# Ten of fourteen float32 LayerNorm tiles transposed by DMA, as two planes of 16 bits

## The chip, the cores and the metric

The kernel runs on one core of one Trainium2 chip. The metric is the time of one execution on the device, in microseconds (us), as a median over runs. A profiled execution gives the trace that the views below are read from: which instruction ran on which engine, and when. The engines are PE (the matrix engine, TensorE, with PEld for its weight loads), DVE (VectorE), ACT (ScalarE), POOL (GpSimd) and SP (SyncE, which here only issues DMAs). Each engine takes its instructions strictly in its own program order, so an instruction that waits holds back everything behind it on that engine.

## The reference: one decoder layer

The input `x` is 8 sequences of 112 tokens with 512 features in float32, 896 tokens together. Three blocks follow one another, each with a LayerNorm before it and a residual sum after it:

```
x = x + attn(layernorm(x))          # 16 heads of 32, causal, rotary q and k, float32
x = x + xattn(layernorm(x), ctx)    # 16 heads, keys and values from ctx (128 features)
x = x + ffn(layernorm(x))           # 512 -> 2 x 2048 -> 512, gelu gate, products in fp8 e4m3
```

with `layernorm(x) = (x - mean) / sqrt(var + 1e-5)` over the 512 features. Of the 375 context rows only the first 112 pass the causal mask, so only these are read.

## The kernel before: seven tiles of tokens, and an order written out

The 896 tokens are seven tiles of 128 rows. A product on PE contracts over the partitions, so the normalized tokens must be turned: a tile of 128 tokens x 512 features becomes four blocks of 128 features x 128 tokens. The result lies in two arrays, `fmh` and `fml`: the value rounded to the format fp32r, and the rest that the rounding left. Each product of the two attention blocks is then three products, high by high, high by low and low by high (`mm3`, line 363).

**LayerNorm.** `ln_stats` (lines 304 to 313) computes mean and variance on DVE, a power of -1/2 on POOL (line 307), and the normalized tile `xn` on ACT (kind "a", before self-attention, line 311) or on DVE (kinds "x", before cross-attention, and "f", before the feed-forward part, line 313). There are seven tiles of each kind, so "a" and "x" make the fourteen float32 tiles of the title.

**Turning a float32 tile.** For "a" and "x", PE multiplies the tile with an identity, four transposes of 128x128 into one bank of PSUM (line 349, tiles `xna` and `xnx`). `split_evac` then takes the bank out: ACT copies and rounds into `fmh` (line 324), and DVE subtracts to give `fml` (line 325).

**Turning an "f" tile.** Kind "f" is fp8 and is turned by a DMA already: `flip` widens to bfloat16 (line 332), SP issues a DMA transpose of 128x512 elements of 2 bytes (line 333, `xt<-xw`), and ACT or DVE narrows the result into `x8` (lines 334 and 335).

**The stages.** First the tiles are normalized and projected to values, queries and keys for tokens 0 to 447 and 448 to 895 (`values`, `proj_fm`, rotation in `rope_evac`). Self-attention runs sequence by sequence: scores on PE (line 420, `pss`), mask and maximum on DVE (429), exponentials with their sums on ACT (432), reciprocals on DVE (435), a scaling on POOL or DVE (436), a transpose of the probabilities on PE (443, `pspt`), a copy (320, `pts`), and the product with the values (453, `psav`). When all sequences of a token tile are through, `finish` does its output projection (`wo`), the residual sum on DVE (466) and the "x" LayerNorm. `cross_kv` makes keys and values of the context, `cross_q` the queries of cross-attention in three groups of tokens, 0 to 383, 384 to 639 and 640 to 895, with the weights `wxq`. Cross-attention has the same steps as self-attention, then `wxo`, the "f" LayerNorm, and the feed-forward part in four groups of tokens (`psfg` line 572, `psfo` line 597).

**The order.** All these steps are first collected in a list and then issued in the order that the string `ORDER` gives by their numbers; a letter behind a number chooses the engine (a ACT, d DVE, p POOL) where a step may run on more than one. So stages overlap as that order has it, and PE works on output projections and context keys between the small products of attention. `CAPS` gives the number of buffers of each kind; the SP queue holds all loads and, further on, the DMAs of the rotation and the transposes.

```
        def tr():
            for c in range(4):
                o, x = ps()[:, c * 128 : (c + 1) * 128], xn()[:, c * 128 : (c + 1) * 128]
                T.transpose(o, x, ident())
        op("pe", tr, r=[xn, ident], w=[ps])
        split_evac(lambda k: fm[k]()[:, :, t0:t1], lambda k: K(fm[k], t0, t1), [ps], psv, 512)
```

Of the kernel before, what the change touches and what calls it, by code (L numbers as in the profile page):

```python
# [8 lines left out]
F32 = mybir.dt.float32  # L9
FR = mybir.dt.float32r  # L10
BF = mybir.dt.bfloat16
F8 = mybir.dt.float8e4
# [19 lines left out]
PAIR = 4  # L32

# [17 lines left out]
class Plan:  # L51
# [47 lines left out]
    "p": 8, "s": 4, "t": 15, "w": 4, "w8": 1, "sm": 12, "m": 4, "pt": 1, "av": 1, "ws": 4, "pts": 7, "fg": 6, "fo":  # L99
    2, "rp": 5, "xn": 3, "f": 5, "cx": 3, "P": 4, "a8": 1, "nw": 20, "warm": 1, "vt": 2,  # L100
}
ORDER = """
1 23-24 37 40 25-26 43 46 85-87 94 22 88 0 89 95-98 2-20 90-91 21 38 103 112 39p 99 41 42p 92 100-101 44 113 104 102
114 105 45d 106 93 107 257-258 272-273 259 274 47 275-276 32 28 49 115 29 311 116 48p 277 260 278 108 50 261 279-282
262 109 263 283 320 51d 312 264-267 55 35 52 36 56 117 110 287 53 73 58 284 111 57d 64 118-119 288-290 268 120 59 54d
321 60d 74 75p 65 27 61 286 269 66d 302 322 62 63d 313 303-304 323 305 67 33 76 30 70-71 68 72p 155 291 156-157
121-122 158 123 159 292 124-129 160 130 161-163 131 189 132 190 164 191 165 293 192 294 193-194 324 134 133 1128 544
34 31 271 285 136 166-167 170 135 195 295 168 69d 196 296 197 297 138-139 198 140 199 141-142 298 200 143 172 202 299
201 144 173 145 174 146-147 175 148 545 77 169 1129 546p 314-315 306 223 176-177 149 178-180 224 240 225 547 82 325
137p 78d 151 150 153 83 316 307 171p 152 204 270 241 181-183 185 184 242 326 226-227 243 228 530 327-328 154d 528-529  # L110
203 187 186 244 229 206 230 245 231-232 246 548 233 207 247 234 248-249 236 235 250 308 208 309 209-210 317 211 318
212-215 310 188d 205p 329 216 251-253 330-333 217 334-335 219 319 218 237-238 254 79 255 220-221 336 465-469 337 470
346-347 338 348-349 339 350-352 340 353 471-472 354 473 355 474 356-357 256d 239d 341-342 222d 380 475 397 476 398 359
80 565 477 84d 358 360 592 361 343 549p 1130p 527 362p 81p 300 363-366 399 580 578 478-479 594 582 608 584 606 566 570
596 367-369 602 604 568 572 590 593 609 567 381 510 382 511 370-371 512 383 372 513-516 373-374 569 573 571 574
375-376 517-521 400 384 401 385 402 607 597 605 579 583 603 522 575d 585 581 591 595 617 576 414 386 586 587p 577a 523
377 301 344 524 378 415 387-388 588 416 403 389 610 618 598 620 622 599d 624 630 611d 634 623 589a 417 390-391 418 600
419 404 420 405-406 421 407 392 636 601d 621 635 619 625 612 422-423 408 424-425 631 626 642 632 393 646 654 637 633
643 613a 658 660 638 648 647 649 659 409-410 345p 627p 379p 639p 431 448 432 628 629a 655 614 394-395 644-645 427 426
650 656 412 428 411 429 640 449 433-434 450 435 615 531 651p 641d 657 661 690 616 721 662 693 663p 652 695 697 691 727  # L120
653a 698 480 436-438 481 439 664 482 451-454 483 455-457 440 458 441-442 484-485 459 731 729 719 709 715 733 707 703
692 665d 696 694 705 699 710 728 722 720 708 732 706 704 525 413p 700d 717-718 701 702a 716 666 763 430p 443-444 711
712p 460 667 723 462-463 550 446 445 668 724p 396p 713 730 734 714a 768 461 735 766 769 486 1139-1141 1142a 788 767
1135 725 726a 736p 1136-1137 1143 487-488 1144-1145 792 764 794 770-771 765 778 776 780 790 1138d 772 489 737 495 490
496 491 497 464p 773p 447p 779 777 738a 804 782 795 800 802 806 783 781 492 793 789 791 784 807 803 801 805 774 739
836 775d 1146d 796 853 855 851 785p 786 797p 841 787d 837 808 498 669 499-500 670 501 798 740 854 852 856 842 849
843-844 838 879 799d 877 875 839-840 880 850 526 809p 671 502 672 503-504 673-675 810 676 505 677 506 678-679 845 873
865 861 811a 846p 867 857 863 741 876 864 874 868 866 878 862 858p 847 909 812 507 848d 912 493-494 508-509 553 556
532 859 916 869 914 928 881 922 870p 917 913 860a 742-743 680 744 926 745 871 746-747 681 910 813 915 927 551 936-937
923 911 872d 934 940 814 924 682 882p 918 748-751 883 752 815 753 816-826 884a 935 925 929 533 754 946-947 941 950 930  # L130
# [49 lines left out]
2131 1971-1972 2125a 2139a 2140 2101 2145 2116 2144 2117-2118 2148d 2146d 2108 2119 1973d 1981p 2120a 2126 2127a 2128  # L180
2147 1974d 2149 2142 2150 2121d 2143 2129 2109 2130 2132d 2133 2134a 2135-2136 2046-2048 2110 2049 2050a 2051d
2111-2112 2113a 2151-2152 2158-2161 2153-2154 2114d 2162a 1982 1975 2115 2122 2045 2163p 2164 2052 2165-2168 2155d
2156d 2169a 2170d 2157 2171
"""
QG = ((0, 4), (4, 8))
XQ = ((0, 384), (384, 640), (640, 896))
# [474 lines left out]
```

## Time and profile before

| | us |
|---|---|
| median of 3 runs | 281.81 (281.14 to 282.51) |
| the profiled execution: its time | 281.24 |
| its span, first to last instruction | 279.3 |
| PE busy | 273.7 (98%) |
| DVE busy | 221.8 (79%) |
| ACT busy | 194.3 (70%) |
| POOL busy | 109.5 (39%) |
| transposes of the float32 tiles, line 349: 56 products | 8.4 busy |
| DMA transposes of the "f" tiles: 7 | 2.4 each from issue to landing |

A busy sum adds the durations of the records of one engine. Matmuls are pipelined, so records of PE overlap, and a PE that shows as busy throughout need not be at its peak: what a product costs is read from the chain of waits, where consecutive products follow each other at the pace at which PE really takes them. The granted clock of PE was 0.998 of full speed over the whole execution.

### The profile page before, as it was taken

What the parts mean: (1) busy time and instruction counts of PE and PEld (TensorE: products, weight loads), DVE (VectorE), ACT (ScalarE), POOL (GpSimd) and SP (SyncE); (2) the same over time, 40 slices, a digit from 0 to 9 for tenths busy, and PEclk for the clock granted to TensorE, in tenths of its full rate; (3) what the DMA queues carried; (4) which work ended last, traced back from release to release, by engine and by line L of the source; (5) the groups of instructions that cost most, each with busy time, mean ns of one, the idle gap of its engine ahead of it and who ended that gap; (6) DMA issues with size and microseconds to landing.
All of it is one profiled execution on the core that took longest, in us unless ns stands there. A gap on an engine that the chain in (4) does not pass through costs nothing.

```text
span 279.3 us, 7540 instructions
## 1 busy us (share of the span) xinstructions
PE 273.7 (98%) x2648; PEld 223.6 (80%) x2648; DVE 221.8 (79%) x909; ACT 194.3 (70%) x697; POOL 109.5 (39%) x123
## 2 busy tenths in 40 slices
PE   8999999999999999999999999999999999999994
PEld 3788988898888888878999887888888887776654
DVE  3896887889988889897897889998967858565372
ACT  3854410787999999970599999999886864633141
POOL 2727680347796398614035454732201200101000
PEclk9999999999999999999999999999999999999999
DMA  7994322332030413016909609410010100001005
GB/s 229 362 339 158 137 104 87 113 129 76 17 104 26 153 40 115 2 35 43 102 9 87 69 3 105 49 38 4 2 40 2 38 2 0 20 1 41 0 38 190
DMA packets 18742, 21.70 MB, mean 78 GB/s; under 512 B 7056, under 2 KB 11536, under 8 KB 18704
## 3 DMA queue, kind: packets, MB, share of 16 engines
q1 hardware_dynamic: 15584, 18.07, 20.1%
q0 software_dynamic: 3120, 3.15, 12.7%
q8 instruction: 21, 0.34, 0.5%
q14 instruction: 17, 0.14, 0.2%
HBM read 22.39 MB, written 1.84 MB: 87 GB/s over the span
## 4 chain that ended last, share of the span: by engine, by line
PE 92%; DVE 4%; ACT 1%; DMA 1%; issue 0%; POOL 0%; POOLq 0%
PE psm L363 44%; PE psfg L572 18%; PE pspt L443 10%; PE psfo L597 9%; PE pss L420 6%; PE psav L453 5%; PE psm L349 2%; DVE fml L325 1%; DMA x_sb<-in_x_dram 1%; DVE wxqwl L283 1%; DVE v_sb L320 0%; DVE lnx L304 0%; ACT xna L311 0%; ACT wvwh L281 0%; DVE xnx L313 0%
## 5 line engine op out<-in xcount | busy, mean ns | idle before, releaser
L432 ACT ACTIVATE P<-P,at 112x112 f32<-112x112 f32 x256 | 96.5, 381 | 8.3 <-DVE at L429 8.1
L436 POOL TENSOR_TENSOR P<-P,at 112x448 f32<-112x448 f32 x52 | 48.5, 938 | 52.6 <-DVE at L435 35.8
L429 DVE CUSTOM_DVE_ANT_0 P<-pss,mask 112x112 f32<-112x112 f32 x256 | 55.7, 265 | 3.5 <-PE pss L420 2.2
L432 ACT ACTIVATION_READ_ACCUMULATOR P<-P,at 112x1 f32 x256 | 48.7, 190 | 0.0
L443 PE MATMUL pspt<-ident,P 112*112 112x112 f32 x256 | 35.9, 262 | 0.0
L443 PEld LDWEIGHTS pspt<-ident,P 112*112 112x112 f32 x256 | 27.5, 133 | 7.6 <-issue 1.2
L572 PE MATMUL psfg<-x,wgwl 128*128 128x256 fp8e4 (+1 forms) x256 | 28.5, 259 | 0.0
L572 PE MATMUL psfg<-x,wgwh 128*128 128x256 fp8e4 (+1 forms) x256 | 28.0, 259 | 0.0
L572 PEld LDWEIGHTS <-wgwl 128*128 128x128 fp8e4 x256 | 21.9, 98 | 5.0 <-issue 1.4
L572 PEld LDWEIGHTS <-wgwh 128*128 128x128 fp8e4 x256 | 22.1, 98 | 4.5 <-issue 0.9
L320 ACT CAST gf<-psfg 128x512 bf16<-128x512 f32 x34 | 18.6, 585 | 9.0 <-PE psfg L572 9.0
L320 DVE CAST gf<-psfg 128x512 bf16<-128x512 f32 x22 | 15.0, 685 | 9.3 <-PE psfg L572 9.3
L582 DVE TENSOR_TENSOR gf<-gf 128x512 bf16<-128x512 bf16 x28 | 12.4, 453 | 12.2 <-ACT gf L580 8.3
L320 ACT COPY pts<-pspt 112x448 f32<-112x448 f32 x36 | 18.9, 526 | 4.2 <-PE pspt L443 2.2
L429 DVE DVE_READ_ACCUMULATOR2_ANT at<- 112x1 f32 x256 | 21.3, 83 | 0.0
L580 ACT ACTIVATE gf<-gf 128x512 bf16<-128x512 bf16 x28 | 16.6, 631 | 5.5 <-DVE gf L320 5.4
L320 DVE COPY pts<-pspt 112x448 f32<-112x448 f32 x28 | 17.3, 617 | 2.2 <-PE pspt L443 2.0
L307 POOL TENSOR_TENSOR lnf<-lnf,mhalf 128x1 f32<-128x1 f32 x7 | 4.1, 585 | 37.0 <-DVE lnf L306 37.0
L420 PE MATMUL pss<-k,q 32*112 32x112 f32 x512 | 16.9, 268 | 0.0
L420 PEld LDWEIGHTS pss<-k,q 32*112 32x112 f32 x512 | 14.0, 172 | 3.1 <-issue 2.0
L320 ACT CAST ob<-psfo 128x512 bf16<-128x512 f32 (+1 forms) x7 | 3.5, 494 | 18.3 <-PE psfo L597 18.3
L597 PE MATMUL psfo<-wlin,a 128*128 128x512 fp8e4 x64 | 15.6, 379 | 0.0
(140 smaller groups left out, 644.4 us busy)
## 6 DMA issues: line engine op xcount, KB each, us to landing
qt<-qs SPq DMA_DIRECT2D x32, 112.0 KB, 2.0
x_sb<-in_x_dram SPq DMA_DIRECT2D x7, 256.0 KB, 4.9
out_dram<-x_sb SPq DMA_DIRECT2D x6, 256.0 KB, 2.3
wst<-in_Wv_dram SPq DMA_DIRECT2D x4, 256.0 KB, 4.9
wst<-in_Wq_dram SPq DMA_DIRECT2D x4, 256.0 KB, 5.1
wst<-in_Wo_dram SPq DMA_DIRECT2D x4, 256.0 KB, 3.7
wst<-in_Wk_dram SPq DMA_DIRECT2D x4, 256.0 KB, 5.1
wst<-in_WoutT_dram SPq DMA_DIRECT2D x4, 256.0 KB, 3.3
```

Source lines behind the costliest of these rows:

```text
L320: lambda e: A.copy(dst(), src()) if e == "act" else V.tensor_copy(dst(), src()), r=r, w=w)
L363: T.matmul(out=out(), lhsT=l(a), rhs=r(b), start=q == 0, stop=q == 3 * tot - 1)
L420: T.matmul(out=banks[r]()[:S, j * S : (j + 1) * S], lhsT=qk[0]()[rs, c, t0 : t0 + S], rhs=qk[1]()[rs, c, t0 : t0 + S], start=True, stop=True)
L429: op("dve", lambda ps=ps, r=r, j=j, Pv=Pv, sm=sm: V.tensor_tensor_reduce(Pv()[:, r, :], ps()[:S, j * S : (j + 1) * S], mask(), -SCALE, BIG ...
L432: op("act", lambda r=r, Pv=Pv, sm=sm: A.activation(Pv()[:, r, :], Pv()[:, r, :], AF.Exp, bias=sm()[:S, r : r + 1], scale=-1.0, accum_out=s ...
L436: op(("pool", "dve"), lambda e, sm=sm, Pv=Pv: LO[e].tensor_tensor(Pv(), Pv(), sm()[:S, 8:12].unsqueeze(2).broadcast_to([S, 4, S]), ALU.mul ...
L443: T.transpose(pt()[:S, r * S : (r + 1) * S], Pv()[:, r, :], ident()[:S, :S])
L453: T.matmul(out=av()[r * 32 : (r + 1) * 32, c * S : (c + 1) * S], lhsT=v_sb()[:, b, h * 32 : (h + 1) * 32], rhs=pts()[:S, r * S : (r + 1) * ...
L572: T.matmul(out=ps()[:, j * n : (j + 1) * n], lhsT=wg()[i][:, c, (m + j) * 128 : (m + j + 1) * 128], rhs=x8()[:, c, t0:t1], start=(c == 0), ...
L580: op("act", lambda gb=gb: A.activation(gb()[:, :w], gb()[:, :w], AF.Gelu_apprx_tanh), w=[(gf, 0)])
L582: op("dve", lambda gb=gb, fb=fb: V.tensor_tensor(fb()[:, :w], gb()[:, :w], fb()[:, :w], ALU.mult), r=[(gf, 0)], w=[(gf, 1)])
L597: T.matmul(out=ps()[:, :wd], lhsT=a8()[:, m, s], rhs=wl()[0][:, m, hs], start=(m == 0), stop=(m == NH - 1))
```

## The change

A new function, `flip_x`, takes the place of the four products for the "a" tiles 4, 5 and 6 and for all seven "x" tiles. The "a" tiles 0 to 3 stay on PE. The DMA transpose is issued on elements of 2 bytes, as in `flip`, so the float32 tile is first split into its low and high halves:

- a copy on POOL or ACT sorts the 1024 halves of each row into two planes (`xl`),
- SP issues one DMA transpose of 128x1024 elements of 2 bytes (`xv`),
- a copy on ACT or DVE interleaves the two planes again to float32 (`xf`),
- a copy on ACT or POOL rounds into `fmh`,
- a subtraction on POOL or DVE gives `fml`.

The line numbers of the changed kernel for these steps are 352, 353, 354, 357 and 358; what was line 363 (`mm3`) is line 390 there.

`ORDER` is another string throughout: the steps that are in both kernels are issued in another sequence, and many that may run on two engines have another one. `FLIP = 0` leaves the second new function, `flip_p`, for the probabilities, without use, and `hl` and `xt` have no buffers.

```diff
+FLIPA = 4
+FLIP = 0
...
 CAPS = {
...
-1 23-24 37 40 25-26 43 46 85-87 94 22 88 0 89 95-98 2-20 90-91 21 38 103 112 39p 99 41 42p 92 100-101 44 113 104 102
...
+23 1 85-87 22 88 0 25 103 89 104-107 40 90 41 42p 2-18 91 19-21 108-109 24 43-44 94-97 45p 92 37 27 46 38 28 26 55 36
...
     def tmp(name, dt=F32, extra=()):
-        return Buf(("t", *extra), lambda k: sb.tile([128, 512], dt, tag=f"t{k['t']}", name=nm(name)))
+        return Buf(("t", *extra), lambda k: sb.tile([128, 1024 if dt == U16 else 512], dt, tag=f"t{k['t']}", name=nm(name)))
...
+    LO2 = {"act": A.copy, "dve": V.tensor_copy, "pool": G.tensor_copy}
...
+    def planes(t):
+
+        return t.bitcast(U16).rearrange("p (n two) -> p two n", two=2)
...
+    def flip_x(i, xn):
+
+        t0, t1 = i * 128, (i + 1) * 128
+        xl, xt, xf = tmp("xl", U16), tmp("xv", U16), tmp("xf")
+        two = lambda t: t().rearrange("p (two n) -> p two n", two=2)
+        op(("pool", "act"), lambda e: LO2[e](two(xl), planes(xn())), r=[xn], w=[xl])
+        op("sp", lambda: nc.sync.dma_start_transpose(xt().rearrange("p (g s) -> p g s", g=8), xl()), r=[xl], w=[xt])
+        op(("act", "dve"), lambda e: LO2[e](planes(xf()), two(xt)), r=[xt], w=[xf])
+        src = lambda: xf().rearrange("p (c s) -> p c s", c=4)
+        hi, lo = (lambda: fm[0]()[:, :, t0:t1]), (lambda: fm[1]()[:, :, t0:t1])
+        op(("act", "pool"), lambda e: LO2[e](hi(), src()), r=[xf], w=K(fm[0], t0, t1))
+        op(("pool", "dve"), lambda e: LO[e].tensor_tensor(lo(), src(), hi().bitcast(F32), ALU.subtract),
+           r=[xf, *K(fm[0], t0, t1)], w=K(fm[1], t0, t1))
+
     def layernorm(i, kind):
         xn = ln_stats(i, kind)
         if kind == "f":
             flip(i, xn)
+            return
+        if kind == "x" or i >= FLIPA:
+            flip_x(i, xn)
             return
```

## The prediction

> **What bounds the kernel now.** I read the page's busy sums first, then the chain of waits, then tables of busy time by stage, and last the groups of the instructions that the change takes away or resembles.
>
> ```profile
> PE 273.7 (98%) x2648; PEld 223.6 (80%) x2648; DVE 221.8 (79%) x909; ACT 194.3 (70%) x697; POOL 109.5 (39%) x123
> ...
> PE 92%; DVE 4%; ACT 1%; DMA 1%; issue 0%; POOL 0%; POOLq 0%
> ```
>
> A busy PE proves little by itself, but the chain says the same: 92% of the span is PE following PE. So a product less on PE is time less, as far as nothing else comes up in its place. What is next shows in the stages (columns: stretch, its length, then busy time with instructions of PE, PEld, DVE, ACT and POOL, clock, DMA share, GB/s):
>
> ```profile
> 47.50:107.20 59.70, 59.70 (x686) 50.09 (x686) 53.12 (x302) 53.24 (x241) 38.58 (x39) 1.00 0.24 77
> 107.20:121.00 13.80, 13.80 (x137) 11.12 (x137) 12.89 (x59) 13.27 (x53) 8.10 (x10) 1.00 0.26 75
> 121.00:136.00 15.00, 14.69 (x113) 13.18 (x113) 12.36 (x24) 3.91 (x8) 4.09 (x5) 1.00 0.57 43
> 136.00:190.20 54.20, 54.20 (x716) 47.22 (x716) 48.90 (x296) 52.92 (x240) 24.22 (x28) 1.00 0.53 54
> ```
>
> The first two rows are self-attention, the third is the passage to cross-attention, the fourth is cross-attention up to its last block of scores. In both attentions ACT, with its exponentials, is nearly as full as PE: 52.92 of 54.20 us in the fourth. In the passage it does almost nothing, 3.91 of 15.00. This matters because the change puts work on ACT. The passage in the chain, in order of time (start, length, what):
>
> ```profile
> 124.57 0.61 DVE lnx L304
> 125.18 0.02 issue
> 125.21 0.18 DVE lnx L305
> 125.39 1.41 DVE wxqwl L283
> 126.80 0.60 DVE fml L325
> 127.40 0.61 DVE wxqwl L283
> 128.01 0.04 issue
> 128.05 7.04 PE psm L363 x39
> 135.09 0.87 PE psm L349 x8
> 135.96 0.98 PE pss L420 x32
> ```
>
> From 118.09 to 128.05 the chain runs through DVE, but PE was not empty there: its records leave 0.31 us idle in the passage. Then the products with `wxq`, eight of the transposes in question in 0.87 us, and the first cross-attention scores.
>
> **Part 1: the products that go.** Ten tiles of four transposes are 40 products of line 349. Their record is 272 to 277 ns long, but records overlap; in the chain eight take 0.87 us, four take 0.44, so 0.109 us each: 40 x 0.109 = 4.36 us off PE. The groups:
>
> ```profile
> L349 PE MATMUL psm<-ident,xna 128*128 128x128 f32 x28 | 4.2, 272 | 0.0
> L349 PE MATMUL psm<-ident,xnx 128*128 128x128 f32 x28 | 4.2, 277 | 0.0
> L324 ACT CAST fmh<-psm 128x512 fp32r<-128x512 f32 x14 | 7.9, 581 | 4.3 <-PE psm L349 4.3
> L325 DVE TENSOR_TENSOR fml<-psm,fmh 128x512 fp32r<-128x512 f32 x14 | 9.6, 686 | 1.0 <-ACT fmh L324 0.9
> ```
>
> All other PE products are the same in number and shape in both programs. The Trainium skill speaks against the change here: "VectorE: DVE Perf Modes", section "Rules for kernel authors", says to transpose 128x128 on TensorE if a result in PSUM will do, and by DMA otherwise; its section on the three transpose paths gives 390 ns for the one and 1309 ns for the other. By that figure 40 products would weigh 15.6 us (an estimate from that page), not 4.36; the rule compares single latencies, while the rows above give the pace within a stream.
>
> **Part 2: what comes onto the other engines.** Counted in the instruction order of the changed program, the ten tiles get 10 plane copies out (8 ACT, 2 POOL), 10 back (8 ACT, 2 DVE), 10 roundings (3 ACT, 7 POOL), 10 subtractions (7 POOL, 3 DVE). No row shows a copy of 1024 elements of 16 bits with a step of two. ACT takes 586 ns for 512 elements and 265 for 128 (line 320, `ob`), so 0.836 ns per further element; from 615 ns for 512 out of SBUF (line 281) that gives 615 + 512 x 0.836 = 1043 ns. Bounds: 615 ns if halves go two at a time, 2.1 us if the step doubles the price. I take 1.04, since 16-bit rows (`xw`, 617 ns for 512) cost per element what 32-bit rows do.
> - ACT: 16 x 1.04 + 3 x 0.62 - 10 x 0.58 = +12.7 us; other steps reassigned to or from it sum to about +0.4. So 194 to 207 of 279 us.
> - DVE: -10 x 0.69 + 3 x 0.69 + 2 x about 1.1 = -2.6; reassigned steps -0.8.
> - POOL: 7 subtractions at 1.3 (line 283), 7 roundings between 0.66 (line 332) and 1.3, two plane copies between 0.66 and 2.6: +15 to +23, taken +18; reassigned steps +4. 109 to 131 us.
> - SP: ten transposes. The 128x512 ones take 1.19 us to issue and 2.4 to land. Twice the size: 2.4 at least, 4.8 at most; I take 3.5, as the 1.2 us behind the issue need not double.
>
> **Part 3: where that lies.** (a) Tiles a4 to a6. Their transposes are at SP rows 20, 28 and 32, amid the Wk loads. PE wants these tiles for tokens 448 on, some 29 us of products behind its first, so 3.5 us more of latency is covered; ACT is busy 20.56 of the first 47.00 us, so 6 long copies (6.2 us) fit. If the cover failed, the Wk loads queued behind a waiting transpose would come late; the first Wk product stands 16.7 us of products into the stream. I cost it nothing.
> (b) Self-attention. ACT gets the plane copies of x0 and x1, 2 x 1.04 = 2.1 us, ahead of exponentials. Of its 59.70 - 53.24 = 6.5 us idle, 5.4 is one wait at the start, so 1.1 is left. What exceeds it is 1.0 us (0 to 2.1 at the bounds for the copy being hidden or not at all); half should be lost later in slack before the passage: +0.5.
> (c) The passage. In x5 and x6 the chain from the last residual sum is: DVE 0.69 + 0.69 + 0.18 + 0.15, POOL 0.55, DVE 0.54, plane copy 1.04, DMA 3.5, copy back 1.04, rounding about 0.7: 9.1 us, to about 10 with two tiles in one queue. Between that tile's last output projection and its first `wxq` product, PE has group 0 (48 products at the 0.18 of "7.04 ... x39", 8.7 us), a block of scores (0.98) and 34 to 36 products of group 1 at 0.12 (4 us): 13.7 us. Covered, with 3 to 4 us to spare. ACT gets 8.3 us of long copies here and has 11.1 idle. Cost 0, bounds 0 to 3.
> (d) Cross-attention. No new work on ACT, but ACT has 1.3 us spare. Work on PE ahead of the first cross scores falls by nine groups of transposes (3.9 us) and rises by products moved up, to 2.8 less, so the first exponential comes 2.8 us earlier, and PE's remaining 1.6 us of gain falls into a stage where ACT can follow it no further than its spare 1.3. Lost: 0 to 1.6, taken 0.8, half.
>
> **Sum.** The profiled execution's own time is 281.24, its span 279.3 and 1.94 around it. 281.24 - 4.36 + 0.5 + 0.8 = **278.2 us**, 1.1% less. The median of the runs shown, 281.81, is 0.57 above that execution; 278.2 stands for either within this.
>
> **Rivals.**
> 1. The whole gain arrives and the new sequence also fills ACT's and PE's small waits: the bounds in (b) and (d) at zero give 276.9; a further 1.1 us of ACT's 1.3 to 6.5 us idle gives 275.8. For it: DVE's chain piece of 10 us is relieved by 2.6 to 3.4 us. Against: PE had only 0.31 us idle there.
> 2. The chain through memory is late: transposes at 4.8 us and POOL copies at 2.6 use up the spare 3 to 4 us of (c), and (b) and (d) at their bounds add 2.1 and 1.6: 280.6 if (c) stays at 0, 283.6 with its bound of 3. I take 281, no change. For it: POOL takes plane copies, roundings and subtractions of x2 to x6 in one row. Against: DMA share in the passage is 0.57.
> 3. Slower: ACT's copies decide. At 2.1 us instead of 1.04, the passage gets 8 x 1.04 = 8.3 us more on ACT where (c) left 2.8, so 5.5 us late; and x0 and x1 put 4.2 us ahead of exponentials with 1.1 to spare, so 3.1. 281.24 - 4.36 + 5.5 + 3.1 = 285.5. With c the price of a copy, 8 (c - 1.04) - 2.8 + 2 c - 1.1 equals the 4.36 gained at c = 1.66 us, the point from which it decides. For it: no row has a step of two 16-bit elements. Against: the price per element of 16 and 32 bits is alike in `xw`.
>
> **Numbers.** Forecast 0.48, rival 1 0.18, rival 2 0.18, rival 3 0.16. The range 275.5 to 283.0 holds the forecast, rivals 1 and 2, and the milder part of 3. What a measurement of this kernel tells from no change is about 0.5%, so faster means under 279.8 by this execution: 0.18 + most of the forecast (0.42) + little of rival 2 (0.03) = 0.63; same 0.06 + 0.13 + 0.02 = 0.21; slower 0.16.
>
> **What the changed profile would show.** Line 376 (the transposes kept) with 16 products instead of 56; ACT's `xl` and `xf` at about 1.04 us each (over 1.66: rival 3); `xv` landing in 3.5 us; the first cross scores 2.8 us or more earlier, at about 133; ACT over 98% between first and last cross scores. I would be wrong if PE waited for `fmh` or `fml` from POOL in the passage, or if the self-attention stretch grew.

## The result, and the profile after

The changed kernel takes 292.16 us (median of 4 runs, 290.09 to 293.56); the kernel before, run beside it on the same chip, 281.48 us (280.81 to 282.51). The ratio is 1.037, with a 95% interval of 1.030 to 1.044: slower by 10.7 us where 3 us less was forecast. The profiled execution of the changed kernel took 290.09 us, its span is 288.3 us, 9.0 more than before. All that follows reads from that one.

The page of the changed kernel, busy sums and chain of waits:

```profile
PE 274.2 (95%) x2608; PEld 220.3 (76%) x2608; DVE 222.8 (77%) x904; ACT 208.2 (72%) x706; POOL 130.4 (45%) x139
...
PE 65%; DVE 12%; ACT 10%; DMA 7%; issue 3%; SPq 1%; POOL 0%; ACTq 0%; DVEq 0%; POOLq 0%
```

PE has its 40 products less (2608 instead of 2648), though its busy sum rose by 0.5 us, and the sums of ACT and POOL rose about as predicted. What changed is the chain: PE fell from 92% of it to 65%, and in its place stand DVE, ACT and DMA. The busy sums do not tell this, the chain does.

The table by stage (stretch, length, busy time of PE, PEld, DVE, ACT and POOL, clock, DMA share, GB/s): self-attention to its last scores, the rest of it, the passage, cross-attention to the scores of its seventh sequence, and from there to the scores of the eighth.

```profile
48.50:108.70 60.20, 59.06 (x679) 48.45 (x678) 54.35 (x301) 53.28 (x237) 40.09 (x41) 1.00 0.31 83
108.70:122.50 13.80, 12.66 (x122) 9.38 (x122) 12.96 (x60) 13.65 (x58) 8.95 (x10) 1.00 0.40 98
122.50:137.90 15.40, 15.33 (x111) 13.37 (x110) 11.79 (x22) 11.13 (x17) 9.83 (x11) 1.00 0.42 84
137.90:183.70 45.80, 44.62 (x587) 38.46 (x586) 41.34 (x251) 44.23 (x199) 26.84 (x30) 1.00 0.67 60
183.70:199.10 15.40, 10.82 (x97) 8.86 (x92) 8.81 (x46) 9.95 (x43) 2.48 (x3) 0.89 0.63 51
```

The last row is where most is lost: 15.4 us between two blocks of scores that lie 9.1 apart before (181.1 and 190.2), with every engine idle for part of it and DMA busy. In the passage ACT is no longer nearly empty: 11.13 us of 15.40, where it was 3.91 of 15.00. The groups of the new steps (a row's columns as before):

```profile
L376 PE MATMUL psm<-ident,xna 128*128 128x128 f32 x16 | 2.4, 272 | 0.0
L352 ACT COPY xl<-xnx 128x1024 uint16<-128x1024 uint16 x5 | 5.2, 1048 | 4.2 <-DVE xnx L319 4.0
L354 ACT COPY xf<-xv 128x1024 uint16<-128x1024 uint16 x8 | 10.9, 1366 | 0.2 <-DMA xv<-xl 0.2
L358 POOL TENSOR_TENSOR fml<-xf,fmh 128x512 fp32r<-128x512 f32 x7 | 9.7, 1388 | 0.3
```

A copy into two planes costs 1.05 us, one back 1.37; the ten transposes land in 3.0 to 5.0 us, median 3.2 (from the view of the tile `xv`). The copy back is the one price that is clearly off, by 0.33 us. The starts of some of the 16 blocks of scores (eight of self-attention, eight of cross-attention) in the profiled executions say where each kernel of this study gains and loses:

| kernel | 1st | 8th | 9th | 11th | 15th | 16th | span |
|---|---|---|---|---|---|---|---|
| before | 47.5 | 107.1 | 135.9 | 150.1 | 181.1 | 190.2 | 279.3 |
| after | 48.5 | 108.7 | 137.9 | 152.9 | 183.7 | 199.1 | 288.3 |
| e1 order alone | 49.5 | 109.2 | 143.3 | 158.9 | 189.7 | 204.0 | 292.9 |
| e2 turned tiles alone | 59.6 | 120.2 | 159.9 | 185.5 | 216.6 | 225.7 | 315.0 |
| e4 before, late loads | 47.5 | 107.1 | 135.9 | 150.1 | 181.1 | 197.2 | 286.2 |
| e5 gate loads early | 49.2 | 108.5 | 137.7 | 156.8 | 187.6 | 197.5 | 286.8 |
| e6 Wk loads first | 48.1 | 107.2 | 136.5 | 151.6 | 183.6 | 198.2 | 287.5 |
| e9 both loads | 47.7 | 107.0 | 136.2 | 151.3 | 182.1 | 191.3 | 280.5 |
| e14 e9 with products | 49.8 | 109.7 | 143.8 | 159.4 | 190.2 | 199.6 | 288.5 |

Of the 9.0 us the kernel loses 6.3 between the 15th and 16th block, 1.1 up to the first, and 0.5, 0.4 and 0.7 in self-attention, the passage and cross-attention; the tail takes the same time. The 1.1 us are hardly more than one execution differs from another: e18 below has the start of the kernel before, and its first block comes at 48.5 where that one's comes at 47.5.

**The last block.** The chain of the changed kernel there (start, length, what):

```profile
183.34 8.53 DMA xt<-xw
...
191.89 0.42 ACT x L344
...
192.43 0.62 ACT x L344
...
193.09 1.26 PE psfg L615 x8
```

The first two "f" tiles, which a DMA turned already before, take 8.53 and 7.6 us to land instead of 2.4. What else the queues carried then is in the timeline of POOL, which issues the loads of the feed-forward weights (wgwh, wgwl and wlin; SP issues all other loads). The two loads of the gate weights, first in the kernel before, then in the changed kernel:

```profile
145.88 0.84 POOL L509 DMA_DIRECT2D wgwh<-in_wgat_dram  x1
...
165.52 0.81 POOL L509 DMA_DIRECT2D wgwl<-in_wgat_dram  x1
```

```profile
166.35 0.81 POOL L552 DMA_DIRECT2D wgwh<-in_wgat_dram  x1
...
172.60 0.80 POOL L552 DMA_DIRECT2D wgwl<-in_wgat_dram  x1
```

The new order issues these two loads of 1 MB 20 and 7 us later. Before, wgwl lands after 13.5 us, at 179.0, and the first xt is issued at 180.5. In the changed kernel wgwl needs 18.7 us, to 191.3, and the xt issued at 183.3 land right after it. ACT stands at the head of its queue waiting for xt, and PE waits 4.31 us for ACT.

The slow transposes are not all of it: the first feed-forward products read wgwl itself. PE's weight loads of them, first in the kernel before, then in the changed kernel:

```profile
L572 PEld LDWEIGHTS <-wgwl 128*128 128x128 fp8e4 x256 | 21.9, 98 | 5.0 <-issue 1.4
```

```profile
L615 PEld LDWEIGHTS <-wgwl 128*128 128x128 fp8e4 x256 | 22.7, 99 | 9.3 <-DMA wgwl<-in_wgat_dram 2.8
```

The 2.8 us are one wait, for wgwl to land. It ends at 191.35, and the products start at 193.09. So with transposes in time they would still have stood until 191.35, and the transposes add 1.7 us.

**The start.** The chain of the changed kernel has SP's queue and a Wk load in it, which the chain of before has not:

```profile
18.66 0.42 SPq L261
...
19.14 0.45 SPq L261
...
19.63 4.69 DMA wst<-in_Wk_dram
...
24.34 0.62 ACT wkwh L287
24.96 0.96 ACT xl L352
```

SP's timeline shows the transpose of a4 issued at 14.68, after a wait since 11.8 for its plane copy, and the four Wk loads behind it at 16.12 to 21.54. Before, they were issued at 10.98 to 17.38.

### The profile page after: what moved, and what is told of

The parts are those of the page before. It is cut to its first block, busy times and chain, and to the rows that moved or that the text cites. A ratio compares the mean times of both kernels' runs of the same rounds, so it can differ in the third digit from the quotient of the medians.

```text
span 288.3 us, 7523 instructions
## 1 busy us (share of the span) xinstructions
PE 274.2 (95%) x2608; PEld 220.3 (76%) x2608; DVE 222.8 (77%) x904; ACT 208.2 (72%) x706; POOL 130.4 (45%) x139
## 4 chain that ended last, share of the span: by engine, by line
PE 65%; DVE 12%; ACT 10%; DMA 7%; issue 3%; SPq 1%; POOL 0%; ACTq 0%; DVEq 0%; POOLq 0%
PE psm L390 27%; PE psfg L615 18%; PE psfo L640 8%; PE pspt L486 6%; ACT P L471 4%; DVE P L468 3%; DMA xt<-xw 3%; PE pss L459 3%; PE psav L496 3%; DMA wst<-in_Wk_dram 2%; DMA wst<-in_WoutT_dram 2%; ACT xl L352 1%; ACT xf L354 1%; DMA x_sb<-in_x_dram 1%; DVE xnx L319 1%
## 5 line engine op out<-in xcount | busy, mean ns | idle before, releaser
L475 POOL TENSOR_TENSOR P<-P,at 112x448 f32<-112x448 f32 x48 | 45.6, 952 | 54.7 <-DVE at L474 42.0
L486 PE MATMUL pspt<-ident,P 112*112 112x112 f32 x256 | 36.6, 265 | 2.5 <-DVE pts L326 1.1
L615 PE MATMUL psfg<-x,wgwl 128*128 128x256 fp8e4 (+1 forms) x256 | 29.8, 265 | 4.3 <-ACT x L344 4.3
L615 PEld LDWEIGHTS <-wgwl 128*128 128x128 fp8e4 x256 | 22.7, 99 | 9.3 <-DMA wgwl<-in_wgat_dram 2.8
L326 DVE COPY pts<-pspt 112x448 f32<-112x448 f32 x30 | 18.5, 615 | 7.8 <-PE pspt L486 7.4
L326 DVE CAST gf<-psfg 128x512 bf16<-128x512 f32 x26 | 17.6, 685 | 8.3 <-PE psfg L615 8.3
L326 ACT CAST gf<-psfg 128x512 bf16<-128x512 f32 x30 | 16.8, 581 | 7.4 <-PE psfg L615 7.4
L326 ACT COPY pts<-pspt 112x448 f32<-112x448 f32 x34 | 17.8, 524 | 4.5 <-PE pspt L486 4.2
L625 DVE TENSOR_TENSOR gf<-gf 128x512 bf16<-128x512 bf16 x28 | 11.6, 420 | 7.4 <-ACT gf L623 5.7
L496 PE MATMUL psav<-pts,v_sb 112*32 112x112 f32 x512 | 15.8, 262 | 0.3 <-ACT pts L326 0.3
```

The source lines that it names most:

```text
L326: lambda e: A.copy(dst(), src()) if e == "act" else V.tensor_copy(dst(), src()), r=r, w=w)
L475: op(("pool", "dve"), lambda e, sm=sm, Pv=Pv: LO[e].tensor_tensor(Pv(), Pv(), sm()[:S, 8:12].unsqueeze(2).broadcast_to([S, 4, S]), ALU.mul ...
L486: T.transpose(pt()[:S, r * S : (r + 1) * S], Pv()[:, r, :], ident()[:S, :S])
L496: T.matmul(out=av()[r * 32 : (r + 1) * 32, c * S : (c + 1) * S], lhsT=v_sb()[:, b, h * 32 : (h + 1) * 32], rhs=pts()[:S, r * S : (r + 1) * ...
L615: T.matmul(out=ps()[:, j * n : (j + 1) * n], lhsT=wg()[i][:, c, (m + j) * 128 : (m + j + 1) * 128], rhs=x8()[:, c, t0:t1], start=(c == 0), ...
L625: op("dve", lambda gb=gb, fb=fb: V.tensor_tensor(fb()[:, :w], gb()[:, :w], fb()[:, :w], ALU.mult), r=[(gf, 0)], w=[(gf, 1)])
```

## Experiments

My theory after the result: the places of the loads in the new order cost most, not the copies and transposes. The rival: the copies and transposes cost it by themselves. All kernels are set up from the changed one, with `ORDER` edited, unless it says otherwise. In the diffs of `ORDER` the numbers are steps, and only the neighbourhood is shown. Each ratio is to the kernel before, run beside it on the same chip.

### 1. The two halves of the change apart

The new order with all ten tiles turned by products; each of the three steps of a tile stands at or near the place of its counterpart. PSUM's four banks forced some shifts, of up to 61 steps in an order of some 2,200; all other steps keep their sequence.

```diff
-        if kind == "x" or i >= FLIPA:
+        if (kind, i) in FLIPS:          # FLIPS = []
```

> The changed kernel's sequence of steps, but with all ten tiles turned by products with the identity again (4 transposes of line 376 for each), each set beside its old place in the new sequence. Theory (the new sequence itself is dear, because its feed-forward weight loads wgwh and wgwl start at 166 and 173 us where they started at 146 and 166): the wait for xt behind wgwl, about 6 us, stays, the 4.36 us of products come back, and what the copies and transposes cost goes: 286 to 290 us. Rival (the planes' copies and transposes by themselves cost the time, and the sequence is harmless): 280 to 283 us.

294.54 us, ratio 1.0449 (1.0423 to 1.0475): the new order without any turned tile is no faster than the changed kernel. The theory's part on the last block holds (14.3 us between the last two score blocks). The size was above my range, because the passage takes 34.1 us here instead of 29.2: PE is idle there for 3.6 us instead of 1.2, in waits of up to 1.5 us.

The old order with all ten tiles turned by DMA:

> The sequence of the kernel before, every load at its old place, but all ten tiles turned by DMA as in the changed kernel, with the same engines; the plane copy and the transpose stand right behind the normalized tile, the copy back at the place of the old transposes. Theory (the loads' new places cost most): 278 to 284 us, 4.36 us of products saved and some waits of PE for fmh and fml because the old sequence left 2 us for the way that takes 7 to 9. Rival (the copies and transposes cost what was lost): 289 us or more.

315.79 us, ratio 1.1213 (1.1189 to 1.1237). Here the theory missed widely: the rival's condition came true. The groups show where:

```profile
L390 PE MATMUL psm<-fmh,wxqwh 128*128 128x256 f32 (+1 forms) x48 | 12.4, 334 | 9.6 <-POOL fmh L357 9.6
...
L390 PE MATMUL psm<-fmh,wqwh 128*128 128x448 f32 x32 | 10.8, 401 | 9.5 <-POOL fmh L357 9.5
```

PE waits 9.5 us at the a tiles and 9.6 at the last x tiles for the copy chain, with 9.4 more at other places behind ACT. With these waits the mean granted clock of its four runs was 0.944 to 0.946, so part of the 34 us is a slower PE. The way through memory takes about 7.5 us (1.05 + 3.2 + 1.37 + 0.61 + 1.29 by this case's rows), where the products with their two copies out take 1.7 (0.44 + 0.58 + 0.69); it stands open wherever the order leaves a tile no more than that. So turning the tiles by DMA needs another order; neither half of the change stands by itself.

### 2. The feed-forward loads

The three loads moved forward in the new order:

```diff
-... 1425 1410 570 1147p ... 1544 1580d 568 1590p ... 1683 1205a 569 1651p ...
+... 783p 453p 570 675 ... 1456p 567p 568 1338 ... 1544 1580d 569 1590p ...
```

> The changed kernel with only the three loads of the feed-forward weights moved on POOL's queue: wlin from 143.5 us to about 81, wgwh from 166 to about 156, wgwl from 173 to about 166. Theory: the first two xt transposes at 183 us land in 2.4 us instead of 8.5, the 4.3 us wait of ACT and of PE for them goes, and the clock dip behind it: about 6 us less than the changed kernel, 285 to 287. Rival (PE waits for something else at the same place, the loads are only named by the profile): within 1 us of the changed kernel, 290 to 293.

288.95 us, ratio 1.0237 (1.0197 to 1.0277), half of what I expected. The gain is there: xt lands in 4.2 us at most, PE's wait is 0.7 us instead of 4.3, the last two blocks lie 10.1 apart. But wlin, issued at 83 us, runs into the WoutT loads, which land in 6.8 us instead of 3.5 (medians); one of them is 7.3 us of the chain, and the 8th block comes at 113.2 instead of 108.7. So I moved two things where one was meant.

The reverse, in the kernel before, with nothing turned by DMA: the loads late.

```diff
-... 1411 1396p 562 1412p ... 1592 1570p 563 1621 ...
+... 1592 1570p 562 1621 ... 1663 1631p 563 1659 ...
```

> The kernel before, nothing turned by DMA, with only wgwh and wgwl moved later on POOL's queue, from 146 to about 166 us and from 166 to about 172, as the changed kernel has them. Theory: the first feed-forward product with wgwl, at 186.1 us, waits until the load lands at about 191, and xt with it: 285 to 288 us. Rival (other products cover it, or the load is no bound): 281 to 283.

288.92 us, ratio 1.0255 (1.0222 to 1.0288). All its blocks of scores stand where they stood, up to the 15th at 181.1; the 16th comes 7.0 us late. Its groups and its table by 4 us show the same wait and a lower clock behind it:

```profile
L615 PE MATMUL psfg<-x,wgwl 128*128 128x256 fp8e4 (+1 forms) x256 | 29.4, 264 | 4.8 <-ACT x L344 4.8
```

```profile
188.00:192.00 4.00, 0.88 (x5) 0.71 (x6) 2.04 (x13) 1.56 (x7) 0.00 (x0) 0.56 0.62 54
192.00:196.00 4.00, 4.00 (x24) 2.91 (x23) 2.00 (x11) 2.21 (x10) 0.93 (x1) 0.58 0.00 0
```

Two moved loads make the kernel before 7.3 us slower. This is the largest single cause, shown here from one side and by the next run and e9 from the other.

The gate loads alone, in the new order:

```diff
-... 1456p 567p 1338 ... 1544 1580d 568 1590p ... 1683 1205a 569 1651p ...
+... 570 1147p 567p 568 1288 ... 1544 1580d 569 1590p ...
```

> The changed kernel with wlin left where it is (143.5 us) and only the two gate loads moved forward on POOL's queue: the last low part of wxo, which the gate loads wait for, directly behind the last subtraction of the passage, then wgwh at about 148 instead of 166, and wgwl at about 166 instead of 173. Theory (two things were mixed in the kernel with all three loads moved: a gain at the first xt, and a loss where wlin at 82 us slowed the WoutT loads from 3.3 to 6.8 us): the gain alone remains, the last block of scores follows the one before it by about 10 us instead of 15.4, and the time is 284 to 287. Rival (the three loads now overlap one another and come late together, so that xt still waits): 289 to 292.

287.92 us, ratio 1.019 (1.012 to 1.026). The last two blocks lie 9.9 us apart, as expected. But a new wait of 2.33 us came up at 146.1, since POOL now does two subtractions, the low part of wxo and two issues in one row, and DVE is held up beside it (below). The 11th block is 3.9 us later than in the changed kernel.

### 3. The loads at the start

```diff
-... 31 49 272 ... 51d 309 67 271 270 64 32-33 61 310a ... 320 70 285 ...
+... 31 49 67 64 61 70 272 ... 51d 309 271 270 32-33 310a ... 320 285 ...
-    "ws": 4
+    "ws": 8
```

The second edit gives the loads of weights eight staging tiles instead of four; the run does not part the two edits.

> The changed kernel with only the four Wk loads moved on SP's queue ahead of the a4 transpose that stands waiting until 14.7 us, and ahead of the v_sb copies. Theory: the Wk loads issue at about 12 to 14 us instead of 16 to 22, the wait of ACT for Wk at 22.5 to 24.3 goes, the first block of scores comes 1 to 2 us earlier (about 47) and the end with it: 290 to 291. Rival (the start is bound by the chain on ACT and DVE of casts, plane copies and rotations, and the load only looks last): first scores at 48 to 50 as before, time 292 within 0.7.

288.82 us, ratio 1.0244 (1.0185 to 1.0302): 0.0126 less than the changed kernel's 1.037, so about 3.5 us less and more than expected, with 2 to 3 us of uncertainty since both ratios have theirs. The profile shows less: first scores at 48.1 instead of 48.5 and the 8th block 1.4 us earlier. So that the wait costs time is likely, and how much is open. Prediction step (a) named this wait and put it at nothing.

### 4. Two repairs that were none

```diff
-... 500 514-515 499 565 562 538 559 894p ...
+... 500 565 562 559 514-515 499 538 894p ...
...
-... 1069 1243a 1145a 566 ... 1376 1070a 1185p ...
+... 1069 1243a 1145d 566 ... 1376 1070d 1185p ...
```

> The changed kernel with two edits that lie far apart in time: three WoutT loads go on SP's queue ahead of the v_sb copies that wait until 90 us, and the copies back of x5 and x6 (line 354) go from ACT, where they stand at 137.7 and 140.2 us ahead of the first exponentials of cross-attention, to DVE, which is idle there. Theory: the wait of ACT for WoutT at 97 us goes and score block 8 comes about 1 us earlier, and the second cross block comes 1.3 to 2.5 us earlier against the first: 288.5 to 290.5. Rival (ACT is full anyway, and DVE pays for what ACT gains): 292 within 0.7.

Ratio 1.041 (1.032 to 1.050): no gain, if anything worse. The loads did not start earlier (93.1 instead of 92.7 us): with the v_sb copies out of their way they still waited, for the buffers that they fill, which I had not checked; and the v_sb copies, now behind them, went out at 94.5 instead of 90.0. The 8th block is 2.0 us later. In the passage DVE now waits 3.96 us for the transpose of x6, so the copy back of x4 behind it starts at 139.9 instead of 134.0; PE waits 2.13 us for `fmh`, and the 9th block is 4.4 us later. Another copy back, of 1.56 us at 144.1, stands amid the masks of the first cross block. So DVE pays for what ACT gains, as the rival says. The profiled execution is the longest of the four (297.1 us); its clock is lowered only from 197.8 us on, behind the places named here.

All four edits in one kernel (the diffs of e5, e6 and e7 together):

> All the moves of the three kernels before it together: gate loads early, Wk loads first, WoutT loads ahead of the v_sb copies, copies back of x5 and x6 on DVE. All ten tiles are still turned by DMA. Theory (each loss has its own place and adds): about 6 + 1.5 + 1 + 1.5 us less than the changed kernel, 280 to 283, level with the kernel before. Rival (what one move frees is lost at the next bound, as ACT is nearly full in both attentions): 284 or more.

288.64 us, ratio 1.0234 (1.0184 to 1.0283). The rival, at a glance; but the blocks (110.0 at the 8th, 141.6 at the 9th) show the damage of the two bad edits, and the good two still inside.

The two good moves together, with the low part of wxo placed where POOL is idle:

```diff
-... 1418d 1432p 1353 ... 1456p 567p 1338 ...
+... 1418d 1432p 567p 568 1353 ... 1456p 1338 ...
 (and the Wk loads, and 569 at the old place of 568)
```

> The changed kernel with two of the earlier moves together: the four Wk loads ahead of the a4 transpose on SP's queue, and the gate loads early, but the last low part of wxo, which the gate loads wait for, now behind the second scaling of cross-attention on POOL (about 151 us), not at 146, where POOL's row of four long steps held up DVE and PE waited 2.33 us. Theory (the two losses lie apart and add; the edit of the copies back to DVE is what spoiled the sum of all four): 292.2 less 3.3 and less 4 to 6 us, 283 to 285.5. Rival (not additive, the time freed early is lost again in cross-attention): 287 or more.

283.70 us, ratio 1.0071 (1.0047 to 1.0096). The two losses add: of 10.7 us, about 8.4 are gone (1.037 less 1.0071, of 281.5), with no engine's work changed. In the profiles 1.7 us of the gain are there by the 8th block and 6.1 come at the last block of scores. PE's waits of more than 0.25 us sum to 2.9 us instead of 7.5.

### 5. What is left: the tiles, or the order

From here on the kernel e9 is the base. First the last subtractions on another engine:

```diff
-... 1146p 1071p 1072p 1270 ... 570 1147p ...
+... 1146p 1071p 1072d 1270 ... 570 1147d ...
```

> The kernel with gate and Wk loads moved, and besides the subtractions that give fml of x5 and x6 (line 358) on DVE instead of POOL. Theory (DVE is held up while POOL subtracts: DVE's scaling at 144.7 us took 1.96 us beside POOL's subtraction, where 0.61 is usual, then the copy pts and PE's wait of 1.1 us follow): that scaling takes 0.61 again, PE's wait goes, 0.7 to 1.5 us less than the kernel without this edit. Rival (DVE is the fuller engine in cross-attention, two subtractions of 0.68 us each cost what they free): within 0.5 us of it or above.

285.97 us, ratio 1.0138 (1.0116 to 1.0160): the rival. The hold-up itself went, as the theory said. DVE and POOL of the changed kernel, and DVE of this one:

```profile
144.74 1.96 DVE L475 TENSOR_TENSOR P<-P,at 112x448 f32<-112x448 f32 x1
```

```profile
144.93 1.29 POOL L358 TENSOR_TENSOR fml<-xf,fmh 128x512 fp32r<-128x512 f32 x1
```

```profile
144.70 0.61 DVE L475 TENSOR_TENSOR P<-P,at 112x448 f32<-112x448 f32 x1
```

But in DVE's queue the subtraction of x5 now waits 2.48 us for `fmh` from POOL, ahead of the masks and the scaling, and PE waits 2.66 us for that scaling. A wait was exchanged for a longer one.

Then fewer tiles by DMA, in three kernels (their places in the order fitted as in e1):

```diff
-FLIPS = [a4, a5, a6, x0, x1, x2, x3, x4, x5, x6]      # e9
+FLIPS = [a4, a5, a6, x0, x1, x2, x3, x4]              # e12
+FLIPS = [x0, x1, x2, x3, x4, x5, x6]                  # e13
+FLIPS = []                                            # e14
```

> The kernel with gate and Wk loads moved, and besides x5 and x6 turned by products again, so that eight tiles remain turned by DMA; it takes two plane copies (one on ACT, one on POOL), two copies back of 1.36 us from ACT ahead of the first exponentials of cross-attention, and POOL's two roundings and two subtractions of 1.29 us away, and adds 0.87 us of products, two roundings on ACT and two subtractions on DVE. Theory (ACT's copies at 137.7 and 140.2 us delay the first exponentials, and PE waits in the first two cross blocks): 0.5 to 1.5 us less than the kernel without this edit. Rival (what the products take on PE is what comes back, and they wait for the normalized tile): 0.5 us more or worse.

285.12 us, ratio 1.0121 (1.0089 to 1.0153): the rival, 1.4 us worse, though the interval still touches that of e9. ACT is relieved, PE waits 1.36 us for DVE instead.

> The kernel with gate and Wk loads moved, and besides a4, a5 and a6 turned by products again; the seven x tiles stay with DMA. Theory (the start is bound by loads and by the casts on ACT and DVE, not by PE; three plane copies and three copies back, 7.2 us of ACT, were paid there for 1.31 us of PE): first scores no later than 47.7 to 48.2, total 282.5 to 284.5. Rival (PE sets the start, or the banks of PSUM that the products need hold up the projections): first scores 1 us later or more, 285 or above.

285.76 us, ratio 1.0135 (1.0101 to 1.0169), first scores at 49.5: the rival. In this order turning the a tiles by DMA gains 2 us.

> The kernel with gate and Wk loads moved, with all ten tiles turned by products again, each near its old place in the new sequence. It tells what the ten DMA transposes are worth in the sequence made for them, without the two losses of the loads. Theory (most of the 4.36 us of products is given back by ACT, DVE and POOL): 284 to 287, that is 0.5 to 3 us more than with the transposes. Rival (the whole gain arrives there, and what is lost against the kernel before is the sequence's other moves): 288 or more.

290.30 us, ratio 1.0309 (1.0261 to 1.0358): the rival again, 6.6 us more than with the DMA transposes, of which 4.9 are in the passage. Four of my theories on the remaining loss fell in these four runs, and all the same way: the new order fits its DMA transposes, and each single step taken out of it costs more than it gives. (An order made for products from the start was not among them: in e14 only the steps of the tiles were fitted.) Medians, in us:

| | products | DMA transposes |
|---|---|---|
| order of before | 281.5 | 315.8 |
| order of after | 294.5 | 292.2 |
| order of after, gate and Wk loads moved | 290.3 | 283.7 |

Going over to the old order behind the last turned tile, at three points:

```diff
-... 1071p 1072p   (e9's order to its end)
+... 1071p 1072p   (then all steps still left, in the order of the kernel before)   # e15
+... 1410 570 1147p   (the same)                                                   # e16
+... 1471 1472 1523   (the same, right at the scores of the fourth cross block)   # e17
```

> All ten tiles turned by DMA, the new sequence with gate and Wk loads moved up to the copy back of x5 and its rounding (about 141 us), and behind that what is left in the sequence of the kernel before. Theory (the new sequence is needed for the tiles and loses in cross-attention: from the first cross scores the kernel before needs 143.4 us for 1.5 us more of PE's work, this one 144.3): the rest takes about 142 us, total 280 to 282, level with the kernel before or under it. Rival (the seam costs as much, since the two sequences have different steps left at that point): 283.5 or more.

284.11 us, ratio 1.0084 (1.0063 to 1.0105).

> The same with the seam a little later, behind the last subtraction of x6 (about 146 us), so that PE's wait of 1.1 us there stays. Theory: 281 to 283. Rival (the seam costs): 283.5 or more.

285.14 us, ratio 1.0128 (1.0099 to 1.0156).

> The same with the seam behind the scores of the fourth sequence of cross-attention (about 159 us); the gate loads stand as in the kernel with gate and Wk loads moved, up to the first of them. Theory (what is lost in cross-attention is lost in its first two blocks, and from the third on both sequences run alike): 282.5 to 284, as without the seam. Rival (it is lost evenly over cross-attention): 281.5 or less.

283.01 us, ratio 1.0045 (1.0028 to 1.0062). The first two seams cost waits of PE (1.83 us; 1.55 and 0.82). The third is level with no seam (1.0071) within the intervals: from the fourth cross block on both orders run alike. No kernel with turned tiles came below the kernel before.

### 6. Is a product less time less?

The last two take products away in the kernel before and move nothing. They leave out part of the computation: the low part of the weights in the first query group, and that of wxo for five tiles. In `mm3`:

```diff
+                if cut and 0 < q // tot < 2:
+                    return
...
+... cut=w is wxq_ and t0 == 0)      # the passage
+... cut=w is not wo and i < 5)      # cross-attention
```

> The kernel before with less work on PE in the passage to cross-attention and nothing else moved: it leaves out the 16 products of the first query group with the low part of the weights (wxqwl by fmh), 0.17 us each, 2.8 us of PE between 124 and 136 us. Theory (in the passage PE sets the pace, ACT being busy 17.19 of 28.80 us, and what comes earlier out of it stays earlier): first cross scores at 133 to 134.4, total 279 to 280. Rival (the DVE chain of the last residual sum and of wxqwl sets the passage): 281 or more.

279.99 us, ratio 0.9934 (0.9911 to 0.9958). From the 8th to the 9th block 27.0 us instead of 28.8: of 2.8 us off PE, 1.8 arrive. The first cross scores come at 135.1, later than the theory had them, since this execution's first block came 1.0 us later than in the kernel before. DVE's chain of the last tiles decides the rest, and PE waits 1.4 us for `xnx`.

> The kernel before with less work on PE in cross-attention and nothing else moved: it leaves out the products of the output projections of token tiles 0 to 4 with the low part of wxo, 20 of about 0.23 us, 4.6 us of PE between about 150 and 195 us. Theory (ACT with 39.50 of 40.10 us and DVE set the pace there, PE's full share is filler): the last block of scores comes no more than 1 us earlier than at 190.2, total 280 to 281.5. Rival (PE sets the pace, as its full share says): 276.5 to 278.

281.30 us, ratio 0.9979 (0.9961 to 0.9997). PE has 4.6 us less to do, 3.7 of them before the last block of scores (16 of the 20 products; those of tile 4 stand behind it), and that block comes at 189.9 instead of 190.2. The same stretch in the kernel before and in this one:

```profile
150.10:190.20 40.10, 40.10 (x528) 33.79 (x524) 36.39 (x217) 39.50 (x176) 19.75 (x23) 1.00 0.52 56
```

```profile
150.10:190.20 40.10, 38.09 (x519) 31.04 (x520) 36.50 (x217) 39.66 (x177) 19.99 (x23) 1.00 0.53 57
```

ACT had no more than 0.6 us idle in both. PE's full column in the first was filler between exponentials, and the chain showed it as PE because a filler product follows a product. So work that the new order moves ahead of cross-attention frees PE there and gains next to nothing, because ACT sets the pace: e9 takes 40.0 us from the 11th to the 16th block, before 40.1. In self-attention the block starts say the same (59.3 us from the first to the 8th, before 59.6), but no run took products out there.

## Why the prediction was wrong, point by point

The changed kernel took 14 us more than the forecast. Some 8.4 of them go when the gate and Wk loads are moved (e9); the other 5.5 are the forecast gain, 3.3, which does not arrive, and the 2.2 by which e9 stays above the kernel before.

- **"A product less on PE is time less, as far as nothing else comes up in its place."** This step failed. It holds in the passage for 1.8 of 2.8 us and in cross-attention for 0.5 of 4.6. I had the row that says so (ACT 52.92 of 54.20 us) and gave it 0.8 us in (d).
- **Part 1.** The count was right: line 376 has 16 products, PE's total fell by 40.
- **Part 2.** `xl` 1.05 us against 1.04 predicted; `xf` 1.37 against 1.04, the same price taken for both; `xv` 3.2 against 3.5. ACT's sum rose by 13.9, predicted 13.1; POOL's by 20.9, predicted 22. DVE's was to fall by 3.4 and rose by 1.0: its instructions ran about 10 us over the lower quartile of their own line and shape, in the kernel before about 5 (only what exceeds by 0.15 us or more is summed), and each of those that did ran beside an instruction of POOL. I had not priced this hold-up.
- **Part 3 (a), cost nothing.** Failed, and in the very way named: the Wk loads behind a waiting transpose came late. What that cost is open: 3.5 us by the medians of e6, with 2 to 3 us of uncertainty, and 0.5 us at the first scores in its profile. ACT had the time for the copies; SP's queue had none for the wait.
- **(b), +0.5 in self-attention.** The stretch from the first to the 8th block grew by 0.5 us, which I had named as a sign of being wrong; that the size fits the term is luck. ACT's wait of 5.4 us runs from 44.2 to 49.5, so only 2.0 us of it lie in the stretch, and ACT had 4.4 us left for the plane copies, not 1.1. With the same copies on ACT the stretch takes 59.2 to 59.3 us in e5, e6 and e9, less than before. In the changed kernel a WoutT load is 4.33 us of the chain there, and in e5, e6 and e9 none is.
- **(c), nothing in the passage.** It grew by 0.4 us, with work taken off PE. Of the 40 products 24 lay in it (2.6 us), 12 ahead of the first scores and 4 just behind the first cross scores. With the 1.1 us of products moved up, by (d), it was to shrink by 1.5, so the term is about 1.9 us: within its bounds of 0 to 3, but not nothing. The trace has nine other products more in the passage and PE idle for 1.2 us instead of 0.3, and the chain there runs through ACT's copies (`xl` 1.04 us at 120.95, `xf` 1.37 at 123.99), which I had taken for covered. e9 has the same 29.2 us, so the loads are not the reason.
- **(d), 0.8.** From the 9th to the 15th block 45.8 us instead of 45.2, so the gain was lost whole.
- **The sum had no term for the loads.** I worked out the edits to the fourteen tiles, and took the rest of the new order as the old one. Two moved loads were 7.3 us in the kernel before. The order of POOL's DMAs could be read before: wgwh and wgwl moved behind other steps, close ahead of the first feed-forward products, which read wgwl, and of the first xt.
- **The rivals.** Slower had 0.16, for copies at 1.66 us or more; they took 1.05 and 1.37. The side was right in a rival with a mechanism that did not come. First cross scores were to come at about 133; they came at 137.9. ACT was to be over 98% busy between the first and the last cross scores; it was 96.6% up to those of the seventh sequence (44.23 of 45.80) and 88.5% up to the last (54.18 of 61.20). The rule of the Trainium skill that spoke against the change ("VectorE: DVE Perf Modes", section "Rules for kernel authors") is borne out in the old order, 281.5 against 315.8 us, and not in the new one with its loads moved, 290.3 against 283.7; the two times that the prediction took from that page are given there for bf16, where these tiles are float32.

What stays open: which steps of the mended new order hold back the last 0.7%. The profiles place 0.9 us of it in the first two cross blocks and 0.4 in the passage, but no single change found there gained.

## What to carry to other kernels

When a change comes with a new order, list first what moved that the change does not name, the large loads above all, and give each its landing time against the first step that waits for it or for anything in flight with it. Before counting work taken off the busiest engine as time, ask in each stage which other engine is within a few per cent of it: an engine filled with work that can wait shows 100% and gives next to nothing back. A way that is four times as long as the one it replaces can be the better one in an order made for it, so the halves can't be priced apart. No kernel here with turned tiles was faster than the kernel before, though.

## What the runs showed of the hardware

**A wait of PE can cost more than itself.** After single waits of 1.83 (e15), 2.33 (e5), 2.66 (e11) and 4.31 us (the changed kernel) the mean granted clock fell to between 0.50 and 0.85 in the 4 to 8 us behind them; after single waits up to 1.49 us it did not, after two of 1.55 and 0.82 close together (e16) it did (0.51 and 0.63). The length alone does not decide it: after a wait of 2.13 us in e7, at 139.3, the clock stayed full. The kernel with gate loads early, around its wait of 2.33 us (clock is the third column from the right):

```profile
144.00:148.00 4.00, 2.06 (x39) 1.55 (x38) 3.59 (x4) 2.58 (x14) 3.98 (x4) 0.96 0.55 35
148.00:152.00 4.00, 3.54 (x18) 3.57 (x19) 3.29 (x27) 2.13 (x9) 1.49 (x3) 0.50 1.19 96
152.00:156.00 4.00, 4.00 (x29) 3.85 (x31) 1.87 (x9) 3.14 (x15) 0.40 (x1) 0.69 1.23 107
```

At 4 us times what the clock is short of 1, these rows lose up to 0.2, 2.0 and 1.2 us, more than the wait (an estimate). One run of that kernel, at a full mean clock, took 284.42 us, the three others, at 0.988 to 0.994, 287.59 to 288.56. The Trainium skill, "TensorE: Matmul & The Clock Gate", Part 1, "What's actually happening", has the clock halved after an idle window of about 3.4 us; the half is what the row of 0.50 shows, but 1.83 us of waiting was enough in e15. The lowered stretches that end before the kernel does last 3.41, 6.83 or 10.24 us in the clock records of these traces.

**DVE's scaling stood still beside POOL.** With two inputs from SBUF it took 1.96 us beside POOL's subtraction, 3.18 us beside two POOL steps in a row (e5) and 0.61 with POOL idle, and ended about 0.5 us after POOL did. The Trainium skill, "SBUF — State Buffer", section "SBUF: two separate sides", calls the pair of ports that both use an exclusive lock for a whole instruction. The size agrees, as 0.61 and 1.29 make 1.90 us; but the page gives the lock to the one that starts first, and by the records DVE had started 0.19 us ahead of POOL.

**Transposes by DMA landed late beside a large load.** The same 128x512 transpose landed in 2.4 us with the queues free, in 8.53 us beside a 1 MB load, and in up to 9.3 in e4. Two such loads, issued 6 us apart, took 13.0 and 18.7 us.
